# Cutting the last store of a row-product kernel so that one DMA engine gets fewer of its packets

## The chip, the cores and the metric

The kernel runs on one core of a Trainium2 chip. The metric is the device time of one execution in microseconds (us), the median of several runs. A profile of one execution, and its trace, belong to the kernel; times inside it count from the start of the profiled span. The core has 16 DMA engines, which move data between the on-chip memory (128 partitions) and the device's main memory. Work is given to them by the sync engine's queue.

## The reference

For each of 4096 rows of 256 numbers, the products of all pairs `i <= j` are written out, 32896 of them in a row:

```python
def reference(r_inputs):                     # (4096, 256) float32
    d = r_inputs.shape[1]
    dot = jnp.einsum('bi,bj->bij', r_inputs, r_inputs)
    iu, ju = jnp.triu_indices(d)
    return dot[:, iu, ju]                    # (4096, 32896) float32
```

The input is 4.19 MB and the output 539 MB, so that the kernel is almost only a store.

## The kernel before

Each of the 128 partitions holds 32 rows of the input. They are worked through two rows at a time (`REPEAT`), and the 32896 columns in three pieces (`PIECES`) of 10944, 10976 and 10976. A piece is computed into one of two places in on-chip memory (`PLACES`) by VectorE and ScalarE together, and then stored. Six pieces, which are two groups of two rows, are one pass of a loop (`PASS`); there are eight passes. The first two pieces of a pass (`AHEAD`) are issued at the end of the pass before.

```python
    borders = even_borders(0, width, PIECES)
    spans = list(zip(borders, borders[1:]))
    ...
    x_out = out.rearrange("(p h q r) c -> h q p r c", p=P, q=rounds, r=REPEAT)
    ...
    places = [pool.tile([P, REPEAT, slot], F32, name=f"o{k}") for k in range(PLACES)]
    ...
    def take(engine, sem, value: int):
        engine.wait_ge(sem, value).then_inc(sem, -value)
```

Before VectorE writes into a place it takes that place's semaphore `free`, which stands at 16 when all DMA engines have finished the store that last read it. It then lets ScalarE go (`go`), and both report when done (`v_done`, `a_done`):

```python
            if not ahead:
                take(nc.vector, free[p % PLACES], 16)
                nc.vector.sem_inc(go, 1)
```

The sync engine takes both reports and issues the store of the piece, over 128 partitions, two rows and all its columns:

```python
    def sync(h, pieces: range, ahead: bool):
        for p in pieces:
            place = places[p % PLACES]
            parts = list(blocks(p, ahead))
            for lo, hi, *_, base in parts:
                take(nc.sync, v_done, 1)
                take(nc.sync, a_done, 1)
                to = x_out[bass.ds(h, 1), p // PIECES, :, :, base + lo : base + hi]
                nc.sync.dma_start(to.rearrange("o p r c -> p (o r) c"), place[:, :, lo:hi]).then_inc(
                    free[p % PLACES] if len(parts) == 1 else head, 16
                )
    ...
            pieces_of(h, range(AHEAD, PASS), False)
            with engine.If(h < passes - 1):
                pieces_of(nc.s_assert_within(h + 1, 0, passes - 1), range(AHEAD), False)
    ...
    for k in range(PLACES):
        take(nc.sync, free[k], 16)
    for sem in loaded:
        take(nc.sync, sem, 16)
```

The last lines are the end of the program: it waits for the stores from both places and for the loads.

Of the kernel before, what the change touches and what calls it, by code (L numbers as in the profile page):

```python
# [12 lines left out]
P = 128  # L13
UNIT = 32
REPEAT = 2
PIECES = 3
PLACES = 2
SETS = 4
PASS = 6
AHEAD = 2  # L20


BUDGETS = [0.85, 0.85, 0.85]
FIRST = [512, 1536, 3584, 6400]


def even_borders(lo: int, hi: int, pieces: int) -> list[int]:
# [4 lines left out]
def runs(d: int, lo: int, hi: int) -> list:  # L32


    found, at = [], 0
    for i in range(d):
        a, b = max(at, lo), min(at + d - i, hi)
        if a < b:
            found.append((i, i + a - at, a, b - a))
        at += d - i  # L40
    return found
# [42 lines left out]
def split(block: list, budget: float) -> int:  # L84


    scalar, k = 0.0, 0
    while k < len(block):
        scalar += REPEAT * (184 + 0.837 * block[k][3])
        if vector_time(block[k:]) <= budget or scalar > vector_time(block[k + 1 :]):  # L90
            break
        k += 1
    return k
# [7 lines left out]
def kernel(  # L101
# [14 lines left out]
    nc = tc.nc  # L116
# [4 lines left out]
    passes = groups // rounds  # L121
# [3 lines left out]
    spans = list(zip(borders, borders[1:]))  # L125
# [3 lines left out]
    x_out = out.rearrange("(p h q r) c -> h q p r c", p=P, q=rounds, r=REPEAT)  # L129
# [6 lines left out]
    places = [pool.tile([P, REPEAT, slot], F32, name=f"o{k}") for k in range(PLACES)]  # L136
    ctx.enter_context(tc.tile_critical())  # L137

    def semaphore(name: str):
        return ctx.enter_context(nc.semaphore(name))  # L140

    free = [semaphore(f"free{k}") for k in range(PLACES)]
    head, v_done, a_done, go = (semaphore(s) for s in ("head", "v_done", "a_done", "go"))
    loads = [0, each, groups // 2 * each, groups * each]
    loaded = [semaphore(f"loaded{k}") for k in range(len(loads) - 1)]

    def take(engine, sem, value: int):
        engine.wait_ge(sem, value).then_inc(sem, -value)  # L148
# [6 lines left out]
    def blocks(p: int, ahead: bool):  # L155

        lo, hi = spans[p % PIECES]
        cuts = [lo, *(FIRST if ahead and p == 0 else []), hi]
        for a, b in zip(cuts, cuts[1:]):
            block = runs(d, a, b)  # L160
            k = split(block, 0.0 if ahead else BUDGETS[p % PIECES] * REPEAT * (b - a))
            yield a - lo, b - lo, block[:k], block[k:], lo
# [40 lines left out]
    def scalar(h, pieces: range, ahead: bool):  # L203
# [29 lines left out]
        for sem, count in ((a_own, done), (go, turns)):  # L233
            if count:
                nc.scalar.sem_inc(sem, -count)  # L235

    def sync(h, pieces: range, ahead: bool):
        for p in pieces:
            place = places[p % PLACES]
            parts = list(blocks(p, ahead))  # L240
            for lo, hi, *_, base in parts:
                take(nc.sync, v_done, 1)
                take(nc.sync, a_done, 1)
                to = x_out[bass.ds(h, 1), p // PIECES, :, :, base + lo : base + hi]
                nc.sync.dma_start(to.rearrange("o p r c -> p (o r) c"), place[:, :, lo:hi]).then_inc(
                    free[p % PLACES] if len(parts) == 1 else head, 16
                )

    def all_pieces(engine, pieces_of):
        pieces_of(0, range(AHEAD), True)  # L250
        if engine is not nc.sync:
            for sem in loaded[1:]:
                engine.wait_ge(sem, 16)
        kind = engine.engine
        with nc.Fori(
            0,
            passes,
            engines=OrderedEngineSet([kind]),
            head_slot={kind: 0} if engine is not nc.sync else {},
        ) as h:  # L260
            pieces_of(h, range(AHEAD, PASS), False)
            with engine.If(h < passes - 1):
                pieces_of(nc.s_assert_within(h + 1, 0, passes - 1), range(AHEAD), False)

    for (lo, hi), sem in zip(zip(loads, loads[1:]), loaded):
# [4 lines left out]

    take(nc.gpsimd, head, 16 * (len(FIRST) + 1))
    nc.gpsimd.sem_inc(free[0], 16)
    for engine, pieces_of in ((nc.vector, vector), (nc.scalar, scalar), (nc.sync, sync)):
        all_pieces(engine, pieces_of)
    for k in range(PLACES):
        take(nc.sync, free[k], 16)
    for sem in loaded:
        take(nc.sync, sem, 16)

# [26 lines left out]
```

## Time and profile before

| what | value |
|---|---|
| time, median of 3 | 1272.22 us (1272.18 to 1272.31) |
| span of the profiled execution | 1270.1 us |
| VectorE busy | 896.2 us |
| ScalarE busy | 632.1 us |
| moved by the DMA engines | 543.22 MB, mean 428 GB/s |
| stores of a whole piece | 32 of 10976 KB, 15 of 10944 KB |
| from issue to landing of such a store, median | 33.0 us |

The page of the profile gives busy time for each engine, and the span in 40 equal slices in which a digit is the busy share in tenths. For DMA the digit is the mean over the core's 16 engines, so that a single engine at work while fifteen stand idle hardly shows in it. The same view can be taken of a short window, again in 40 slices; each packet is then counted in the slice in which it starts. A packet is one contiguous run of bytes that one DMA engine moves; in a whole piece's store it is one row of the piece. The update of a semaphore is a packet of 4 bytes. In the timeline, "SPq" is the sync engine's queue, "DVE" VectorE and "ACT" ScalarE; square brackets hold the idle time in front of a group and what ended it.

### The profile page before, as it was taken

How to read it: one execution, taken by the hardware profiler on the slowest of the kernel's cores; microseconds unless marked ns; L12 is line 12 of the kernel's file. 1: busy time of each engine (PE TensorE's matmuls, PEld its weight loads, DVE VectorE, ACT ScalarE, POOL GpSimd, SP SyncE). 2: the span in 40 equal slices, each digit the busy share in tenths (PEclk: the TensorE clock that was granted, in tenths of full speed). 3: DMA queues.
4: the chain of work that ended last, by engine and by line, in shares of the span. 5: the costliest groups of instructions: out<-in, count | busy, mean ns of one | idle time of the engine just before them, and what ended most of it. 6: DMA issues, size and time to landing. Idle time of an engine off the chain costs nothing. (4 is left out here: it accounts for less than half of the span.)

```text
span 1270.1 us, 4343 instructions
## 1 busy us (share of the span) xinstructions
DVE 896.2 (71%) x1733; ACT 632.1 (50%) x1897; POOL 0.2 (0%) x4
## 2 busy tenths in 40 slices
DVE  8867776777667776677757776677766777577760
ACT  8635635455364543645437453374534735257350
POOL 0000000000000000000000000000000000000000
DMA  9999999999999999999999999999999999999997
GB/s 380 437 440 426 437 440 422 441 422 440 422 441 421 440 423 439 430 432 439 424 437 424 439 423 440 422 440 425 437 428 433 422 442 420 441 421 441 421 420 336
DMA packets 14582, 543.22 MB, mean 428 GB/s; under 512 B 880, under 2 KB 880, under 8 KB 1520
## 3 DMA queue, kind: packets, MB, share of 16 engines
q1 hardware_dynamic: 14576, 543.17, 99.4%
q14 instruction: 6, 0.05, 0.0%
HBM read 4.19 MB, written 538.97 MB: 428 GB/s over the span
## 5 line engine op out<-in xcount | busy, mean ns | idle before, releaser
L189 DVE TENSOR_TENSOR o<-xv 128x752 f32<-128x752 f32 (+62 forms) x1716 | 889.3, 605 | 329.3 <-DVEq L148 328.6
L213 ACT ACTIVATE o<-xa 128x253 f32<-128x253 f32 (+58 forms) x1880 | 620.8, 423 | 593.4 <-DVEq L177 593.2
L169 DVE COPY xv<-x 128x512 f32 (+1 forms) x16 | 6.8, 427 | 9.0 <-DVEq L201 4.2
L208 ACT ACTIVATE xa<-x 128x512 f32 (+1 forms) x16 | 10.1, 630 | 5.6 <-ACTq L235 3.9
L208 ACT ACT_TABLE_LOAD x1 | 1.3, 1283 | 4.0 <-DMA x<-in_r_inputs_dram 4.0
L267 DVE MEMSET xv<- 128x1 f32 x1 | 0.1, 59 | 1.0 <-SPq L137 1.0
L293 POOL MEMSET const-bfloat16-1.0<- 128x1 bf16 x1 | 0.1, 102 | 0.0
L293 POOL MEMSET const-uint8-127<- 128x1 uint8 x1 | 0.1, 102 | 0.0
L293 POOL MEMSET const-float32-1.0<- 128x1 f32 x1 | 0.1, 99 | 0.0
L293 POOL MEMSET const-float32-0.0<- 128x1 f32 x1 | 0.1, 98 | 0.2 <-issue 0.2
## 6 DMA issues: line engine op xcount, KB each, us to landing
out_dram<-o SPq DMA_DIRECT2D x32, 10976.0 KB, 33.0
out_dram<-o SPq DMA_DIRECT2D x15, 10944.0 KB, 32.9
out_dram<-o SPq DMA_DIRECT2D x1, 4544.0 KB, 18.7
out_dram<-o SPq DMA_DIRECT2D x1, 2816.0 KB, 14.1
x<-in_r_inputs_dram SPq DMA_DIRECT2D x1, 2048.0 KB, 12.3
out_dram<-o SPq DMA_DIRECT2D x1, 2048.0 KB, 11.6
x<-in_r_inputs_dram SPq DMA_DIRECT2D x1, 1792.0 KB, 6.9
out_dram<-o SPq DMA_DIRECT2D x1, 1024.0 KB, 10.0
```

What stands on the lines that cost most here:

```text
L169: ins = nc.vector.tensor_copy(xv[:, :each], x_of(h, p // PIECES))
L189: ins = nc.vector.tensor_tensor(place[:, :, at : at + m * length], window(xv[:, j:], [[d, REPEAT], [1, m], [1, length]]), window(xv[:, i:] ...
L208: nc.scalar.activation(xa, x_of(h, p // PIECES), AF.Copy).then_inc(a_own, 1)
L213: nc.scalar.activation(place[:, r, at - lo : at - lo + length], xa[:, r * d + j : r * d + j + length], AF.Copy, scale=xa[:, r * d + i : r ...
L267: nc.vector.memset(xv[:, each:], 0.0)
L293: nc = _bacc.Bacc("TRN2", target_bir_lowering=False, num_devices=1)
```

## The change

The store of the very last piece is taken out of the loop and into a function `finish`. It stores the piece's columns in two parts. The first part, all but the last 5408 columns (`LIGHT`), goes out in one store over all partitions as before. The last 5408 columns go out in seven stores: both rows of partitions 16 to 127; both rows of partitions 0 to 2, of 3 to 5 and of 6 to 8; the first row of partitions 9 to 15; and the second row of partitions 9 to 11 and of 12 to 15. Together they cover each row of each partition once. The purpose is that one of the DMA engines gets ten packets of these columns where an ordinary store would give it 16, and others get somewhat more. All eight stores count on one semaphore, `tail`, for which the program waits at its end. What is computed stays as it was.

```diff
@@ -22,6 +22,17 @@
 
 BUDGETS = [0.85, 0.85, 0.85]
 FIRST = [512, 1536, 3584, 6400]
+
+
+
+LIGHT = 5408
+SHARES = [
+    (range(16, 128), range(2)),
+    *((range(p, p + 3), range(2)) for p in (0, 3, 6)),
+    (range(9, 16), range(1)),
+    (range(9, 12), range(1, 2)),
+    (range(12, 16), range(1, 2)),
+]
 
 
 def even_borders(lo: int, hi: int, pieces: int) -> list[int]:
@@ -140,7 +151,8 @@
         return ctx.enter_context(nc.semaphore(name))
 
     free = [semaphore(f"free{k}") for k in range(PLACES)]
-    head, v_done, a_done, go = (semaphore(s) for s in ("head", "v_done", "a_done", "go"))
+    head, tail = semaphore("head"), semaphore("tail")
+    v_done, a_done, go = (semaphore(s) for s in ("v_done", "a_done", "go"))
     loads = [0, each, groups // 2 * each, groups * each]
     loaded = [semaphore(f"loaded{k}") for k in range(len(loads) - 1)]
 
@@ -234,17 +246,34 @@
             if count:
                 nc.scalar.sem_inc(sem, -count)
 
+    def store(h, p: int, lo: int, hi: int, part=slice(0, P), rows=slice(0, REPEAT)):
+
+        base = spans[p % PIECES][0]
+        to = x_out[bass.ds(h, 1), p // PIECES, part, rows, base + lo : base + hi]
+        return nc.sync.dma_start(
+            to.rearrange("o p r c -> p (o r) c"), places[p % PLACES][part, rows, lo:hi]
+        )
+
     def sync(h, pieces: range, ahead: bool):
         for p in pieces:
-            place = places[p % PLACES]
             parts = list(blocks(p, ahead))
-            for lo, hi, *_, base in parts:
+            for lo, hi, *_ in parts:
                 take(nc.sync, v_done, 1)
                 take(nc.sync, a_done, 1)
-                to = x_out[bass.ds(h, 1), p // PIECES, :, :, base + lo : base + hi]
-                nc.sync.dma_start(to.rearrange("o p r c -> p (o r) c"), place[:, :, lo:hi]).then_inc(
-                    free[p % PLACES] if len(parts) == 1 else head, 16
-                )
+                store(h, p, lo, hi).then_inc(free[p % PLACES] if len(parts) == 1 else head, 16)
+
+    def finish():
+        p = PASS - 1
+        ((lo, hi, *_),) = blocks(p, False)
+        take(nc.sync, v_done, 1)
+        take(nc.sync, a_done, 1)
+        store(passes - 1, p, lo, hi - LIGHT).then_inc(tail, 16)
+        for part, rows in SHARES:
+            store(
+                passes - 1, p, hi - LIGHT, hi, slice(part.start, part.stop), slice(rows.start, rows.stop)
+            ).then_inc(tail, 16)
+        take(nc.sync, free[1 - p % PLACES], 16)
+        take(nc.sync, tail, 16 * (1 + len(SHARES)))
 
     def all_pieces(engine, pieces_of):
         pieces_of(0, range(AHEAD), True)
@@ -252,14 +281,18 @@
             for sem in loaded[1:]:
                 engine.wait_ge(sem, 16)
         kind = engine.engine
+
+        end = PASS - 1 if engine is nc.sync else PASS
         with nc.Fori(
             0,
             passes,
             engines=OrderedEngineSet([kind]),
             head_slot={kind: 0} if engine is not nc.sync else {},
         ) as h:
-            pieces_of(h, range(AHEAD, PASS), False)
+            pieces_of(h, range(AHEAD, end), False)
             with engine.If(h < passes - 1):
+                if end < PASS:
+                    pieces_of(h, range(end, PASS), False)
                 pieces_of(nc.s_assert_within(h + 1, 0, passes - 1), range(AHEAD), False)
 
     for (lo, hi), sem in zip(zip(loads, loads[1:]), loaded):
@@ -272,8 +305,7 @@
     nc.gpsimd.sem_inc(free[0], 16)
     for engine, pieces_of in ((nc.vector, vector), (nc.scalar, scalar), (nc.sync, sync)):
         all_pieces(engine, pieces_of)
-    for k in range(PLACES):
-        take(nc.sync, free[k], 16)
+    finish()
     for sem in loaded:
         take(nc.sync, sem, 16)
 
```

## The prediction

> **What bounds the kernel now.** I read the page first: the busy shares, the forty slices and the queue table.
>
> ```profile
> span 1270.1 us, 4343 instructions
> ...
> DVE 896.2 (71%) x1733; ACT 632.1 (50%) x1897; POOL 0.2 (0%) x4
> ...
> DMA  9999999999999999999999999999999999999997
> ...
> q1 hardware_dynamic: 14576, 543.17, 99.4%
> ```
>
> Both compute engines have slack and the DMA queue has none: its packets fill 99.4% of sixteen engines' span. Only the last slice is below 9, so I went to the end with the timeline.
>
> ```profile
> 1209.55 26.75 SPq L245 DMA_DIRECT2D out_dram<-o  x2
> 1216.68 18.40 ACT L213 ACTIVATE o<-xa 128x98 f32<-128x98 f32 x62 [14.91 <-DVEq L177]
> 1216.73 18.82 DVE L189 TENSOR_TENSOR o<-xv 128x468 f32<-128x468 f32 x61 [7.55 <-DVEq L148]
> ```
>
> VectorE ends the last piece at 1216.73 + 18.82 = 1235.55 us. The second issue of the merged row ends at 1209.55 + 26.75 = 1236.30; after it nothing is left but the last store. The 7.55 us idle in front of VectorE's piece is the wait on line 148 for a free buffer, which needs every DMA engine's share of an earlier store. Then the DMA view of 1261 to 1269 us, in slices of 0.2 us:
>
> ```profile
> DMA  5905000000005000000050000000500000000000
> GB/s 220 3073 0 220 0 0 0 0 0 0 0 0 220 0 0 0 0 0 0 0 220 0 0 0 0 0 0 0 220 0 0 0 0 0 0 0 0 0 0 0
> DMA packets 35, 0.83 MB, mean 104 GB/s; under 512 B 16, under 2 KB 16, under 8 KB 16
> ```
>
> This view decides. A packet is one row of the piece, 10976 x 4 = 43904 B, and the view books it where it starts: 220 GB/s over 0.2 us is one packet, 220 + 3073 fifteen. So fifteen engines start their last packet together at about 1261.2 to 1261.35, and the sixteenth starts four more alone, at 1261.8, 1263.4, 1265.0 and 1266.6. (The 16 packets under 512 B are the store's completions, one for each engine.) The lone ones are 1.62 us apart: that is a packet's time, 43904 B / 1.62 us = 27.1 GB/s for one engine. Fifteen engines finish at about 1261.35 + 1.63 = 1263.0 us and one at 1266.65 + 1.63 = 1268.3, which is 5.3 us late. Another 1.8 us to the end of the span is receipt and closing.
>
> That engine was as late before the last store began. The same view from 1236 to 1244 us:
>
> ```profile
> DMA  0000900500009505000099050000990500009905
> GB/s 0 0 0 0 3293 0 0 220 0 0 0 0 3073 220 0 220 0 0 0 0 2854 439 0 220 0 0 0 0 2195 1098 0 220 0 0 0 0 1317 1976 0 220
> ```
>
> 3293 is the fifteen engines starting the last store at 1236.8 to 1237.0, after about 0.3 us without work, because compute had waited for the late engine. The lone 220s are that engine, still in the store before. So one engine is never idle, the others wait for it a little at each piece, and its backlog is the end of the kernel.
>
> [...]
>
> **The change part by part.** The last store is cut at 10976 - 5408 = 5568 columns. The first part is an ordinary 128-partition store, 16 packets of 22272 B per engine. The rest is 256 packets of 21632 B, spread by seven stores. [...]
>
> - [...]
> - three stores of 3 partitions, both rows: 2 x 3 = 6 more on each of engines 0, 1, 2;
> - 7 partitions, one row: 1 on each of engines 0 to 6;
> - 3 and 4 partitions, one row: 1 on each of 0 to 2, and 1 on each of 0 to 3.
>
> [...]
>
> Times, scaled by bytes from 1.62 us: 22272 B take 0.82, 21632 B take 0.80 us; a few hundredths for some dozen more descriptors and completions are in the rounding below.
>
> - Late engine: 16 x 1.62 = 25.9 us becomes 16 x 0.82 + 10 x 0.80 = 21.1. It ends 4.8 us sooner, at 1268.3 - 4.8 = 1263.5.
> - An engine with 17: one short packet more, 0.80, and about 0.1 for its extra completions and packet overheads: 1263.0 + 0.9 = 1263.9 to 1264.0.
>
> The two nearly meet, which is what 5408 columns seem chosen for: 7 packets x 0.80 = 5.6 us against 5.3 late. The end moves from 1268.3 to about 1264.0, so 4.3 us go.
>
> The seven additional issues cost the sync queue about 0.4 us each (my reading of 0.37 us for one issue in the trace, 1235.92 to 1236.30), 2.6 us in all, so they are out by about 1239.5. The engines are busy with the first part until 1236.9 + 16 x 0.82 = 1250. That lies wholly beside other work. Moving the last piece out of the loop changes only the sync queue's program, not compute. Sum: 1272.2 - 4.3 = 1267.9 us.
>
> **Rivals.**
>
> 1. [...] I give this family 25%.
> 2. *112 partitions are cut evenly*, 7 partitions for each of 16 engines[...]. Then engines 0 to 2 have 14 + 6 + 3 = 23, engine 3 has 16, and 1263.0 + 7 x 0.80 = 1268.6: about 1272.6 us[...]. 8%.
> 3. *Another engine is the late one* on this chip. It keeps 16 or 17 packets: 1272.2 to 1273.1 us. 5%.
> 4. *The late engine's backlog differs from run to run.* It was 5.3 us in this trace and the three times lie within 0.13 us, so this moves the result by tenths.
>
> **Range and chances.** Some 62% for the working as meant (1267.3 to 1268.5), the rest from 1272 to 1278, with a long tail. I say 1268.0, and 1267.0 to 1275.0 as the range. 2% is 25 us; nothing I can see in a 26 us store brings that either way.
>
> **What would show it.** The DMA view at the end should have no lone packets, and the last starts of all engines within about 1 us, near 1263. [...] if the even cut holds, three engines run alone for 5 us. If one engine is still alone for 5 us, the light engine wasn't the late one. [...]

## The result and the profile after

The changed kernel takes 1280.57 us (median of 6 runs, 1280.49 to 1280.75) against 1272.17 for the kernel before beside it: 8.4 us more, a ratio of 1.0066 with a 95% interval of 1.0053 to 1.0079. I had predicted 1268.0 us, 4.2 less than before, and a range up to 1275.0. The direction was wrong.

The page of the changed kernel, with the lines that answer to those shown of before:

```profile
span 1278.4 us, 4348 instructions
...
DVE 896.0 (70%) x1733; ACT 632.2 (49%) x1897; POOL 0.2 (0%) x4
...
DMA  9999999999999999999999999999999999999996
...
DMA packets 14878, 543.22 MB, mean 425 GB/s; under 512 B 919, under 2 KB 919, under 8 KB 1559
...
q1 hardware_dynamic: 14871, 543.17, 99.0%
```

Compute and bytes are as before and the span is 8.3 us longer. Queue 1 has 14871 - 14576 = 295 packets more. Cutting each of the last piece's 256 rows in two makes 256 of them; the other 39 are completions. The one last store had 16, so the eight stores have 55. That is the sum 16 + 16 + 3 + 3 + 3 + 7 + 3 + 4: 16 for each of the two large stores, the one over 112 partitions included, and for each small one as many as it has partitions.

The timeline of the last stretch:

```profile
1209.50 33.62 SPq L253 DMA_DIRECT2D out_dram<-o  x9
1216.65 18.40 ACT L225 ACTIVATE o<-xa 128x98 f32<-128x98 f32 x62 [14.92 <-DVEq L189]
1216.70 18.82 DVE L201 TENSOR_TENSOR o<-xv 128x468 f32<-128x468 f32 x61 [7.57 <-DVEq L160]
```

The last piece is computed at the same time as before (1216.70 + 18.82 = 1235.52 us), and all eight stores are issued by 1209.50 + 33.62 = 1243.12. So the loss lies in the transfers after that. The DMA view of 1270 to 1276.3 us:

```profile
DMA  6003060030300033000330003000030000300000
GB/s 275 0 0 137 0 275 0 0 137 0 137 0 0 0 137 137 0 0 0 137 137 0 0 0 137 0 0 0 0 137 0 0 0 0 137 0 0 0 0 0
DMA packets 24, 0.30 MB, mean 48 GB/s; under 512 B 10, under 2 KB 10, under 8 KB 10
```

One packet of 21632 B is 137 GB/s in a slice of 0.16 us. Three engines are still at work at 1270 us, two from about 1272, and one after 1274, each with a packet every 0.80 us. The last packet starts at 1275.4 and ends at 1276.2 us; in the kernel before the last one ended at 1268.3. From there to the end of the span it is 2.2 us, before 1.8. So 7.9 us are transfer and 0.4 us closing.

### The profile page after: what moved, and what is told of

Its sections match the earlier page's. It is cut to its first block, busy times and chain, and to the rows that moved or that the text cites. A ratio compares the mean times of both kernels' runs of the same rounds, so it can differ in the third digit from the quotient of the medians.

```text
span 1278.4 us, 4348 instructions
## 1 busy us (share of the span) xinstructions
DVE 896.0 (70%) x1733; ACT 632.2 (49%) x1897; POOL 0.2 (0%) x4
## 3 DMA queue, kind: packets, MB, share of 16 engines
q1 hardware_dynamic: 14871, 543.17, 99.0%
```

## The experiments

Each is an edit of the changed kernel's list of stores; where a store takes partitions four apart, the step of the range is passed on to it as well. The kernel before took 1272.23 to 1272.27 us beside them. No trace names an engine. In the changed kernel's trace three engines have, after the store over 112 partitions, two packets from each of three small stores and one from each of the other three. So the three completions of a store over 3 partitions come from the same engines each time, and these also take part in the stores over 7 and 4. By this I number the engines: a store over k of at most 8 partitions has the engines 0 to k-1. That the same nesting holds for 5, 6 and 8 partitions is my assumption.

**The cut by itself.** One store over all partitions in place of the seven.

```diff
-SHARES = [(range(16, 128), range(2)), ...six more]
+SHARES = [(range(128), range(2))]
```

> The last 5408 columns go out in one store over all 128 partitions, in place of the seven; the cut into 5568 + 5408 columns and the move out of the loop stay. Theory (the 112 partitions are cut evenly, seven to an engine[...]): the cut alone costs only a second completion, 1272.2 to 1272.5 us, 16 packets of each size on every engine, all short packets near 0.80 us. Rival (shorter packets or the second issue or the changed loop cost the 8 us): 1280 us.

1272.97 us, ratio 1.0006 (0.9997 to 1.0014). The DMA view of 1261 to 1269 us, 0.2 us a slice:

```profile
DMA  0920092002000200020002000200020002000000
GB/s 0 1622 108 0 0 1622 108 0 0 108 0 0 0 108 0 0 0 108 0 0 0 108 0 0 0 108 0 0 0 108 0 0 0 108 0 0 0 0 0 0
DMA packets 55, 0.84 MB, mean 105 GB/s; under 512 B 16, under 2 KB 16, under 8 KB 16
```

It is the picture of the kernel before with half the packet: fifteen engines together (1622), and one alone until 1268.5, its packets 0.80 us apart. That is 0.2 us later than before, and closing takes 2.3 us in place of 1.8. So the second cut and the changed loop account for 0.7 us, where 0.3 at most had been expected, and the seven stores for the rest.

**The store over 112 partitions alone.** The last 5408 columns of partitions 0 to 15 are not stored.

```diff
 SHARES = [
     (range(16, 128), range(2)),
-    *((range(p, p + 3), range(2)) for p in (0, 3, 6)),
-    (range(9, 16), range(1)),
-    (range(9, 12), range(1, 2)),
-    (range(12, 16), range(1, 2)),
 ]
```

> Of the seven stores only the one over partitions 16 to 127 is left; the last 5408 columns of partitions 0 to 15 are not stored. Theory (even cut[...]): every engine has 14 short packets, many of them 1.2 to 2 us long, and the late engine's own long packets are drawn out too[...]. Rival a (even cut[...]): 14 packets of 0.80 us each, the late engine two packets sooner, 1270.6 us.[...]

1275.82 us, ratio 1.0029 (1.0018 to 1.0039), 2.9 above the run before, although an eighth of these columns' bytes is left out (16 of 128 partitions). The DMA view of 1250.6 to 1261.4 us, in which fifteen engines work on this store:

```profile
DMA  1919917919943919957559979579979579795999
DMA packets 175, 3.77 MB, mean 349 GB/s; under 512 B 1, under 2 KB 1, under 8 KB 1
```

The one packet under 512 B is the late engine's completion of its long packets, at about 1260.1. No engine completes the store over 112 in these 10.8 us. The engine that the prediction gives ten packets would have at most ten here, and at 0.80 us each be done by about 1250.1 + 8.0 = 1258.1. The first is done at 1261.5, which is 14 x 0.80 = 11.3 us after the start, and following the packets from end to start the trace has 14 for every engine. The cut is even. But rival a is out: 38 of the 224 short packets take over 1.2 us, where the run before had none over 0.83.

The late engine pays most. Its long packets of 22272 B took 0.83 us each; the last four took 2.00, 2.12, 1.72 and 1.97 us, between 1252.3 and 1260.2, while other engines were at the store over 112. Its share of the long store ended at about 1260.1 us; in the run with the cut alone it ended at 1255.6.

**Two stores over 64 partitions.** All is stored.

```diff
+SHARES = [(range(64), range(2)), (range(64, 128), range(2))]
```

> The last 5408 columns go out in two stores over 64 partitions each, all of them. Theory (even cut: 4 partitions to each of 16 engines[...]): every engine has 16 short packets as in the kernel before, but each takes 1.6 us in place of 0.80, and the end is about 1279.6 us. Rival a (even cut[...]): packets of 0.80 us, 1272.2 us.[...]

1284.07 us, ratio 1.0093 (1.0076 to 1.0110). The DMA view of 1255 to 1263 us, 0.2 us a slice:

```profile
DMA  9900906099500055999000559990005059990050
GB/s 757 436 0 0 216 0 108 0 865 433 216 0 0 0 216 108 541 541 541 0 0 0 216 108 216 757 649 0 0 0 216 0 108 649 757 216 0 0 216 0
```

The starts come in groups 1.7 us apart, where the run with the cut alone has 0.8: the median short packet took 1.68 us. The packets are as large as in that run, where 16 engines x 21632 B / 0.80 us makes 433 GB/s; here it is 16 x 21632 B / 1.68 us = 206 GB/s. A few packets took up to 3.2 us; what brought the time above the expected 1279.6 I have not followed further.

**Which engine is late.** All but the last 512 columns go out as before; these are stored for partitions 0 to 17 only.

```diff
+LIGHT = 512
+SHARES = [(range(5), range(2)), (range(5, 11), range(2)), (range(11, 18), range(2))]
```

> A probe for the number of the late engine. All but the last 512 columns of the last piece go out as before; the last 512 columns are stored for partitions 0 to 4 (5 partitions), 5 to 10 (6) and 11 to 17 (7) only, and not for 18 to 127. If a store over k partitions takes engines 0 to k-1, the late engine, whose packets stand alone at the end, has two packets of 2048 B from each of three stores if it is engine 4, from two if it is 5, from one if it is 6, and from none otherwise. From the trace of the changed kernel, where it had one short packet after its 14 of the store over 112, I expect 4, 5 or 6[...]. The time about 1271.5 us.

1272.03 us in one run, 0.5 over what was expected. The DMA view of 1266.9 to 1267.7 us, where only the late engine is at work:

```profile
DMA  0000002000200020002000020002000000000000
GB/s 0 0 0 0 0 0 103 0 0 0 102 0 0 0 103 0 0 0 102 0 0 0 0 102 0 0 0 102 0 0 0 0 0 0 0 0 0 0 0 0
DMA packets 10, 0.01 MB, mean 15 GB/s; under 512 B 4, under 2 KB 4, under 8 KB 10
```

It has four completions, its long store and three short ones, and six packets of 2048 B. So it takes part in the store over 5 partitions: its number is 4 or less. In the changed kernel its end is this (1274.1 to 1276.4 us):

```profile
DMA  0000000080000000000000800000000000000000
GB/s 0 0 0 0 0 0 0 0 376 0 0 0 0 0 0 0 0 0 0 0 0 0 376 0 0 0 0 0 0 0 0 0 0 0 0 0 0 0 0 0
DMA packets 4, 0.04 MB, mean 19 GB/s; under 512 B 2, under 2 KB 2, under 8 KB 2
```

Two packets, each followed by a completion. The first is the fourteenth of the store over 112, the second its only one from the six small stores. With one packet from the six, by the numbering above, it took part in the store over 7 and in none over 3 or 4, so it is 4, 5 or 6. Both runs together leave engine 4.

**The idea with the right engine.** 544 columns in 32 stores over four partitions, four apart, for engines 0 to 3; engine 4 gets none of them.

```diff
+LIGHT = 544
+SHARES = [
+    *((range(b + q, b + q + 13, 4), range(2)) for b in range(0, 128, 16) for q in range(4)),
+]
```

> What the change was for, with the engine that is late: the last 544 columns go out in 32 stores over four partitions each, four apart (0, 4, 8, 12 and so on), so that they should run on engines 0 to 3 alone[...], and engine 4 gets none of them. Engine 4's sixteen long packets shrink to 10432 columns, 1.28 us less in all. Theory 1[...]: no gain[...], plus up to 0.7 us as in the two-store run. Theory 2 (only the engine is behind): 1271.3 us, plus the same 0.7.

1276.16 us, ratio 1.0031 (1.0019 to 1.0042). That is 3.9 above the kernel before and 4.2 above theory 2 with its 0.7; the timeline of its end says why:

```profile
1209.52 61.89 SPq L249 DMA_DIRECT2D out_dram<-o  x34
1216.70 18.82 DVE L197 TENSOR_TENSOR o<-xv 128x468 f32<-128x468 f32 x61 [7.55 <-DVEq L156]
```

The last issue ends at 1209.52 + 61.89 = 1271.41 us. An issue over four partitions took about 1.29 us while the engines were busy and 0.63 at the end, where I had reckoned 0.4. The last packets had to wait for their issue. The late engine itself was done at 1267.8.

The same without partitions 16 to 31 and 48 to 63:

```diff
-    ... for b in range(0, 128, 16) for q in range(4)),
+    ... for b in (0, 32, 64, 80, 96, 112) for q in range(4)),
```

> As the run before, but the 544 columns of partitions 16 to 31 and 48 to 63 are not stored at all[...]. Engine 4 has the same packets in both. Theory 1[...]: 1.3 us or more below the run before, about 1270.8 us plus up to 0.7. Theory 2 (engine): within some 0.3 us of the run before.

1271.85 us, ratio 0.9997 (0.9988 to 1.0005), with 24 stores. The totals of the two differ by the issue. What I compare is the late engine's sixteen long packets: 25.51 us from first to last in both. The packets of 2176 B from those partitions had not held it up.

At their shortest, 1.54 us, sixteen such packets would take 24.7 us. A part of the difference is here (the same run, 1256 to 1257 us):

```profile
DMA  0000000000000000700000000000900000009999
GB/s 0 0 0 0 0 0 0 0 0 0 0 0 0 0 0 0 328 0 0 0 0 0 0 0 0 0 0 0 1669 0 0 0 0 0 0 0 1669 1669 3338 8346
q14 instruction: 1, 0.01, 1.9%
```

The 328 GB/s at 1256.4 is one instruction packet of 8192 B on queue 14, and it lies exactly in a gap between two packets of the late engine, 1256.40 to 1256.71 (the 1669 at 1256.70 is its next one, which took 1.82 us). This fetch ran on that engine; the two-queue run below has one that did not.

**The same question with large packets.** Eight stores of 2752 columns over four partitions; once of partitions 16 to 31 and 48 to 63, and once of 0 to 15 and 32 to 47. All other partitions' last 2752 columns are left out.

```diff
+LIGHT = 2752
+SHARES = [
+    *((range(b + q, b + q + 13, 4), range(2)) for b in (16, 48) for q in range(4)),   # or (0, 32)
+]
```

> The pair of low4 runs gave the late engine the same end within 0.1 us[...] in packets of 2176 B. Here the same with packets of 11008 B: of the last 2752 columns only partitions 16 to 31 and 48 to 63 are stored, by eight stores over four partitions four apart; the other partitions' are not stored.[...] engine 4's long packets of 1.22 us stretch to about 2.4 us, engine 0's short ones of 0.41 to 0.8, and the end is about 1272.2 us.[...]

> The same number of stores, engines, packets and bytes, but of partitions 0 to 15 and 32 to 47[...]. Both theories: engine 4's long packets stay at 1.22 us, and the end is about 1266.8 us, up to 0.7 more for the second store and the instruction fetch.

1270.61 us (ratio 0.9987, 0.9980 to 0.9994) and 1267.27 us (0.9960, 0.9945 to 0.9975): the same engines, packets and bytes, and 3.3 us between them. The second is at its expectation; the first lies between 1266.8, which is the second's, and its own 1272.2. The DMA view of 1259.3 to 1263.3 us of the first, in slices of 0.1 us:

```profile
GB/s 329 0 330 0 0 110 330 0 0 0 330 0 0 0 330 439 0 0 220 110 0 0 330 110 0 0 220 110 0 0 220 220 0 0 0 0 0 0 0 0
```

And of the second:

```profile
GB/s 0 0 329 330 110 0 0 330 110 0 0 330 110 0 329 330 110 0 0 330 110 0 0 220 220 0 0 0 440 0 0 0 440 0 0 0 0 0 0 0
```

A long packet of 32896 B is 329 GB/s, a short one of 11008 B is 110, and three short ones make 330. In the second run the late engine starts its last two at 1259.5 and 1260.7 (329 each, in slices 3 and 15), 1.23 us apart; it ends at 1262.0. In the first they start at 1259.3 (329) and 1260.8 (in the 439), and the last one takes 2.55 us, to 1263.4. On one of the engines 0 to 3, seven of the short packets took 0.83 to 0.87 us there instead of 0.41. In the first run it is this engine that ends the kernel, not the late one; its last packets, from 1263.3 to 1267.3 us:

```profile
GB/s 110 0 0 0 0 110 0 0 0 110 0 0 0 110 0 0 0 110 0 0 0 110 0 0 0 110 0 0 0 0 0 0 0 0 0 0 0 0 0 0
```

The last one starts at 1265.9 and ends at 1266.3 us. In the second run engines 0 to 3 are done by 1263.0: that is the 3.3 us, while the late engine is 1.4 us later. So it matters which partitions the eight stores read: with 16 to 31 and 48 to 63 the late engine and one other are slower at the same time. That the late engine's own long packets come from there too would fit; no trace shows what partitions an engine reads.

The two are not always equally slow, though. The first run earlier on, 1256.8 to 1260.8 us:

```profile
GB/s 110 329 330 0 110 0 220 110 0 0 220 110 0 439 220 110 0 0 220 110 0 110 220 110 0 329 0 330 0 0 110 330 0 0 0 330 0 0 0 330
```

The late engine starts long packets at 1256.9, 1258.1 and 1259.3 (329, 439, 329); they take 1.22, 1.23 and 1.47 us, the first two at 27 GB/s, while the other engine (the lone 110s, at 1257.2, 1258.9 and 1259.8, and one in the 439) is already at 0.86 us a packet, 12.8 GB/s: 40 GB/s for the two. With the late engine's last packet, 32896 B in 2.55 us or 12.9 GB/s, it is 26. I don't know why the one slows down before the other.

**Neighbours or four apart.** 1376 columns in 16 stores over eight partitions, four apart in the one and next to each other in the other.

```diff
+    *((range(b + q, b + q + 29, 4), range(2)) for b in range(0, 128, 32) for q in range(4)),   # four apart
+    *((range(p, p + 8), range(2)) for p in range(0, 128, 8)),                                 # neighbours
```

> The last 1376 columns go out in 16 stores over eight partitions each, four apart (0, 4, ... 28 and so on): engines 0 to 7, each with 32 packets of 5504 B in place of 16[...]. Both theories: packets of 0.21 us, engines 0 to 7 have 3.3 us more, the late one too: about 1275.7 us.

> As the run before, the same number of stores, engines, packets and bytes, but each store takes eight neighbouring partitions (0 to 7, 8 to 15, ...)[...]. Theory[...]: packets of 0.8 us in place of 0.21 and about 1286 us. Rival[...]: 1275.7 us as the run before.

1276.61 us (1.0034, 1.0019 to 1.0049) and 1279.77 us (1.0059, 1.0040 to 1.0078). Both theories had 1275.7 for the first, and the second lies between 1275.7 and 1286. Neighbours cost 3.2 us more, and not 10: 212 of the 256 short packets took 0.21 to 0.25 us, against 244 with partitions four apart. The late engine's last long packet took 4.39 us in place of 1.45, and that is nearly all of the difference.

**Two queues.** The 32 stores of 544 columns, every second one issued by ScalarE's queue, which waits for the sync engine's signal first and counts on a semaphore of its own.

```diff
+        for k, (part, rows) in enumerate(SHARES):
+            queue, sem = ((nc.sync, tail), (nc.scalar, tail2))[k % 2]
```

> The 32 stores of 544 columns over four partitions, which were held up by an issue time of 1.3 us each on the sync queue, are dealt out in turn to the sync queue and ScalarE's queue, 16 each; everything is stored. If only the engine is behind[...]: the issues end by about 1258 us, engines 0 to 3 end near 1267.5 and engine 4 near 1268.0, and with 0.4 us of longer closing the time is about 1272.0 us, even with the kernel before or 0.3 us under it.[...]

1273.27 us, ratio 1.0008 (1.0000 to 1.0016). The issues ended at 1257.7 us, as expected, but the late engine was not done before 1268.8, and the last of the engines 0 to 3 not before 1269.1, where 1268.0 and 1267.5 had been expected. One of the late engine's long packets took 2.41 us in place of 1.54, and an instruction packet of 0.32 us lay between two others. A second instruction packet was on another engine; from 1248.2 to 1248.7 us:

```profile
GB/s 0 0 0 0 174 0 0 0 0 0 0 655 0 0 0 0 0 0 0 0 0 0 0 0 0 0 0 0 0 0 0 0 0 0 0 0 3338 0 0 3338
q14 instruction: 1, 0.01, 3.9%
q10 hardware_dynamic: 1, 0.00, 1.1%
```

The instruction packet (655, at 1248.34) starts as a short packet of ScalarE's queue (174) ends, and a long packet (the first 3338) starts as it ends. Only engines 0 to 3 have short packets, and the late engine's next long one is the other 3338. No arrangement I ran that stores everything beats the kernel before.

## Why the prediction was wrong

**What held.** The reading of the kernel before: one engine ends it, 5 us after the others. In the changed kernel its share of the last store begins at 1242.3 us, as it did before. Compute and the loop play no part, and the issues were out before 1250, though they took about 1.0 us each and not 0.4.

**The step that failed** is the count of packets behind "10 x 0.80" and "An engine with 17": it needs a store over 112 partitions that gives some engines fewer packets than others. That store was cut evenly, 14 packets on every engine. So no engine had ten; by the numbering above, engines 0 to 2 had 14 + 6 + 3 = 23, engine 3 had 16, engines 4 to 6 had 15, the others 14. No trace of the kernel before has a store over 112 partitions, and I set the even cut aside because it did not give the announced ten. The announcement was no evidence of what the hardware does, and I gave the even cut 8%.

**The second error** is that I took the engine meant to have ten for the late one, although no trace named the late one. It is engine 4, and it got 15 short packets in place of 16.

**The rivals.** The even cut is rival 2, which I put at 1272.6 us. It has the count right, but takes 0.80 us for every short packet. The sum that I should have made is the late engine's own, from 1242.3 us to its last packet's end. Its completion of the long packets, the one packet under 512 B from 1260.1 to 1260.3 us:

```profile
DMA packets 3, 0.04 MB, mean 216 GB/s; under 512 B 1, under 2 KB 1, under 8 KB 1
```

Its 16 long packets thus took 17.9 us, of which 16 x 0.83 = 13.3 are their undisturbed length and 4.6 come on top, much as in the run with the store over 112 alone (2.00 + 2.12 + 1.72 + 1.97 - 4 x 0.83 = 4.5). Its 14 short packets of the store over 112 took 15.2 us, of which 14 x 0.80 = 11.3 are undisturbed and 3.9 on top: the first eight took up to 2.8 us, the last six 0.80 each. One more short packet took 0.8. That makes 33.9 us, where the kernel before had 26.0 (16 x 1.62) and the prediction "16 x 0.82 + 10 x 0.80 = 21.1": 25.4 us of packets in place of 21.1, and 8.5 us on top that it had set at nothing. With 0.4 us of closing this is the 8.3 us of the span.

Of the 3.9 us, the run with the store over 112 alone shows the source: there all 14 took 0.80, so it is the six small stores that held them up. Which seven of the 112 partitions an engine has, and so why eight of its packets were slow and six quick, no trace shows.

**What stays open.** Whether the idea could work at all. It needs other engines to take over the late engine's bytes. Packets of 2176 B from partitions 16 to 31 and 48 to 63 did the late engine no harm (25.51 us for its sixteen long packets with and without them), packets of 11008 B from there did (its end 1.4 us later than with other partitions), and I have no rule for what lies between. Each partition's rows also have one fixed place in main memory, so no run here tells the reading of a partition from the writing to its place. Where the backlog comes from is open too. In the kernel before there is no instruction packet from 126 to 1268 us, and yet the last of a piece's 16 completions, 2.5 us after the first at 143 us, came 5.8 us after it at 1001 us. From 1164 to 1242 us the late engine's packets took 1.636 us on average, the others' 1.629.

## What to carry to other kernels

How many engines share a store depended here on its partitions: as many completions as partitions for 3, 4 and 7, and for 112 fourteen packets on each of 16 engines. With 112 or 64 partitions in place of 128 the packets also took longer (38 of 224 over 1.2 us, and a median of 1.68 us, in place of 0.80). So count the packets of each engine in a trace of the very shape before building on them. When one engine ends a kernel, ask what other stores do while it is still at work: in this kernel relieving it of one short packet in sixteen, 0.80 us, cost 8.4 us. While the engines were busy, small stores also cost the queue more to issue than one large store, 0.95 to 1.3 us against 0.37 to 0.42.

## What I had not expected of the hardware

An instruction packet (8192 B) held up the engine that carried it by 0.31 us, and the packet after it took 1.66 to 1.82 us in place of 1.55; one lay on the late engine, and with two queues one more on one of the engines 0 to 3. Two engines slowed at the same time, in the run with large packets from partitions 16 to 31 and 48 to 63, were not slowed alike: in one stretch 27 GB/s for the late one and 13 for the other, in the next 13 for each.
